# Turning normalized features through HBM instead of inside SBUF, and a bank-to-bank copy in the first gather, in a graph-attention kernel

## The chip, the core and the metric

The kernel runs on one core of one Trainium2 chip. The metric is the device time of one execution in microseconds. A core has five engines with instruction streams of their own: TensorE (PE) for matmuls, VectorE (DVE) and ScalarE (ACT) for element-wise work, GpSimd (POOL) and SyncE (SP). Here SP issues all plain DMAs and all DMA transpositions ("turns" below), and POOL issues the DMAs that add into their destination. All DMAs run on the same 16 DMA engines. SBUF is the on-chip memory, PSUM the matmul accumulators in 8 banks, HBM the memory outside.

## The reference

Inputs are x (32, 512, 512) and an adjacency (32, 512, 512) of integers: 32 samples of 512 nodes with 512 features. One pre-norm layer with two graph-attention (GAT) layers inside:

```python
def gat_layer(x, mask, W, a_src, a_dst, bias, concat):
    B, N, _ = x.shape
    H, F = a_src.shape
    xl = (x @ W).reshape(B, N, H, F)
    asrc = jnp.einsum('bnhf,hf->bnh', xl, a_src)
    adst = jnp.einsum('bnhf,hf->bnh', xl, a_dst)
    e = jax.nn.leaky_relu(asrc[:, :, None, :] + adst[:, None, :, :], NEG_SLOPE)
    e = jnp.where(mask[..., None], e, NEG_INF)
    attn = jax.nn.softmax(e, axis=1)
    out = jnp.einsum('bsdh,bshf->bdhf', attn, xl)
    out = out.reshape(B, N, H * F) if concat else out.mean(axis=2)
    return out + bias

h = jnp.maximum(_layernorm(x, axis=-1), 0.0)
mask = (adj > 0) | jnp.eye(N, dtype=bool)[None]
g = jax.nn.elu(gat_layer(h, mask, W1, att_src1, att_dst1, b1, concat=True))   # 4 heads of 256
x = x + gat_layer(g, mask, W2, att_src2, att_dst2, b2, concat=False)          # 1 head of 512
```

All data are float32.

## The kernel before

A sample goes through these stages: load of x, normalization and relu (`norm`, `norm_turn`), transposition of the normalized features into `ht` (features on partitions), projection with W1 (`project1`, into `xl`), scores and softmax of the four heads (`Soft.first`, `Soft.second`, weights in `p`), the weighted sums over neighbours (`gather1`, into `h1`, then `elu`), projection with W2 (`project2`), second softmax, second gather (`gather2`) and the store. All products of matrices are split into two-by-two blocks and done with seven block products in place of eight; the extra sums of blocks are made on DVE (`sums`, `sums1`, `sums2`, `low_sums`), and the seven products are added up partly inside a PSUM bank and partly by DVE.

The order of instructions is not the order of the code. Every function adds jobs (engine, cost in us, keys read, keys written) to a `Program`; PE's jobs keep the order of the code, and for the other engines the program searches an order with a model of costs, queues and DMA wires, then emits the instructions. SP's queue and POOL's queue are each one stream in that model. A job that turns by DMA has the size `prog.TURN` and is kept from overlapping with POOL's accumulating DMAs in the model (`crossed`). A key is the unit of dependence: a job waits for the last writer of what it reads, and for all readers of what it writes. Buffers come from small sets (`Slots`): four x tiles `xs`, two adjacency tiles `adjs`. `Banks` hands out the 8 PSUM banks; `take(width, kept)` with `kept` over 0 gives a free bank only if its last accumulation was at least that wide, so that a matmul may add to what another engine wrote there, and otherwise gives none.

The main loop (line 1698) runs over the samples, each iteration working on several: first gather of sample i+1 (heads 0 and 1), half of the projection of sample i+2, first gather (heads 2 and 3), the rest of the projection, second gather of sample i, load and norm of sample i+3, second projection of sample i+1, and `norm_turn` of sample i+3. So `ht` of a sample is needed when the next iteration's first half gather is over: `sums(ht_blocks())` and `low_sums()` on DVE read it, and `project1` on PE.

`norm_turn` (line 901) works on one block t of 128 nodes. ACT normalizes with relu in place (x tile `hn`). For samples 0 and 1, PE transposes. For all others the float32 words are split: ACT writes them as 16-bit halves, all low halves and then all high halves, into an adjacency tile (`words`, row adj<-x); SP issues a DMA transposition of 16-bit elements from there back into the x tile (`back`, row x<-adj); and ACT copies from `back` into `ht`, interleaving the halves again (row ht<-x). The same kind of DMA transposition turns the masks (row mt<-m, line 873), with `m` in SBUF as its source.

`gather1` (line 1437) takes two heads at a time in the order `PAIRS_OF`, and in the last iteration one by one in the order `SINGLY`. Product n of head h goes into the accumulator `ACC[n]`: 1, 6, 7 and 4 share bank "a", 5 and 3 bank "b", and 2 has a bank "g" of its own. After products 1, 4, 5, 6 ACT evicts the running sum into `h1` with the bias (row h<-mm,b_sb); after 2, 3, 7 DVE subtracts the bank from `h1` (row h<-h,mm). In `project1` a similar fork already stands: product 1 of the "low" block is copied by ACT into a second bank (row mm<-mm) if `Banks` has one wide enough. All instructions of a helper carry the helper's line: 646 for ACT, 649 for DVE, 652 for SP's plain DMAs, 657 for POOL's, 663 for matmuls.

Of the kernel before, what the change touches and what calls it, by code (L numbers as in the profile page):

```python
# [14 lines left out]
U16 = mybir.dt.uint16  # L15
AF = mybir.ActivationFunctionType
# [4 lines left out]
P = 128  # L21
# [491 lines left out]
def tile_gat(  # L513
# [37 lines left out]
    B, N, D = x.shape  # L551
# [15 lines left out]
    dram = ctx.enter_context(tc.tile_pool(name="dram", bufs=1, space=DRAM))  # L567

    def tiles(name, n, shape, dtype=F32, pool=sbuf):
        return [pool.tile(shape, dtype, name=f"{name}{i}") for i in range(n)]  # L570

    def slots(name, n, shape, dtype=F32, pool=sbuf):
        return Slots(name, tiles(name, n, shape, dtype, pool))
# [25 lines left out]
    ht = sbuf.tile([P, KT, N], F32, name="ht")  # L599
# [12 lines left out]
    ass = slots("as", 2, [P, 2, N])  # L612
    rrs = slots("rr", 2, [P, 2, N])
    das = slots("das", 2, [2 * NT, P], F32, dram)
    drs = slots("drr", 2, [2 * NT, P], F32, dram)
    mds = slots("dm", 3, [P, NT, N], BF16, dram)
    stats = slots("stats", 2, [P, NT, nc.vector.BN_STATS_DIM + nc.vector.BN_AGGR_DIM + 1])
# [2 lines left out]
    banks = Banks(tiles("mm", 8, [P, 512], F32, psum))  # L620
# [18 lines left out]
    def give_p(pk):  # L639
        if pk[0] == "p":  # L640
            ps_.give(pk)
# [3 lines left out]
    def act(cost, reads, writes, *a, **k):  # L645
        prog.add("ACT", cost, reads, writes, lambda: nc.scalar.activation(*a, **k))  # L646

    def dve(cost, reads, writes, f, *a, **k):
        prog.add("DVE", cost, reads, writes, lambda: f(*a, **k))  # L649

    def dma(size, reads, writes, to, at, cost=0.4):
        prog.add("SP", cost, reads, writes, lambda: nc.sync.dma_start(to, at), size)
# [7 lines left out]
    def pe(reads, writes, n, calls):  # L660
        def emit():
            for f, a, k in calls:
                f(*a, **k)  # L663

        prog.add("PE", n, reads, writes, emit)
# [235 lines left out]
    def norm_turn(b, t):  # L901

        (sk, st), (xk, hn) = ST[b], XT[b][t]
        S, A = nc.vector.BN_STATS_DIM, nc.vector.BN_AGGR_DIM
        act(
            0.71, [xk, sk + (t,)], [xk], hn, hn, AF.Relu,
            bias=st[:, t, S : S + 1], scale=st[:, t, S + A : S + A + 1],
        )
        if b < 2:
            pk, pt = banks.take()  # L910
            pe(
                [xk], [pk], 0.44,
                [(nc.tensor.transpose, (pt[:, k * P : (k + 1) * P], hn[:, k * P : (k + 1) * P], identf), {})
                 for k in range(KT)],
            )
            act(
                0.62, [pk], [("ht", t, 0), ("ht", t, 1)], ht[:, :, t * P : (t + 1) * P],
                pt.rearrange("p (k n) -> p k n", n=P), AF.Copy,
            )
            banks.give(pk)  # L920
        else:

            ak, a = adjs.take()
            words = a.bitcast(U16)
            act(
                0.96, [xk], [ak], words.rearrange("p (h f) -> p h f", h=2),
                hn.bitcast(U16).rearrange("p (f h) -> p h f", h=2), AF.Copy,
            )
            back = hn.bitcast(U16)
            prog.add(  # L930
                "SP", 1.3, [ak], [xk],
                lambda: nc.sync.dma_start_transpose(
                    back.rearrange("p (g n) -> p g n", n=P), words
                ),
                prog.TURN,
            )
            act(
                1.21, [xk], [("ht", t, 0), ("ht", t, 1)],
                ht[:, :, t * P : (t + 1) * P].bitcast(U16).rearrange("p k (n h) -> p h k n", h=2),
                back.rearrange("p (h k n) -> p h k n", h=2, n=P), AF.Copy,  # L940
            )
            adjs.give(ak)
        xs.give(xk)
        if t == NT - 1:
            stats.give(sk)
# [160 lines left out]
    M = N // 2  # L1106
# [273 lines left out]
    def sums1(h, pk, p, apart):  # L1380


        def a_block(i, j):
            return (
                xl[:, 2 * j : 2 * j + 2, h, 2 + i * P : 2 + (i + 1) * P],
                [("xl", 2 * j + k, h, i) for k in range(2)],
            )

        def b_block(r, c):
            return (  # L1390
                p[:, 2 * r : 2 * r + 2, c * M : (c + 1) * M], p_keys(pk, (2 * r, 2 * r + 1), (c,))
            )

        a11, a12, a21, a22 = (a_block(i, j) for i in range(2) for j in range(2))
        b11, b12, b21, b22 = (b_block(r, c) for r in range(2) for c in range(2))
        k = KQ + h % 2
        s1, s2 = (
            (hs[:, i, k, :].rearrange("p (k f) -> p k f", f=P), [("hs", i, k)]) for i in range(2)
        )
        s4 = s2  # L1400
        if apart:
            s4 = (hs4[:, h % 2, :].rearrange("p (k f) -> p k f", f=P), [("hs", 2, h % 2)])
        t1, t2 = (
            (t.rearrange("p (k f) -> p k f", f=M), [q]) for q, t in (ts_.take() for _ in range(2))
        )

        def op(cost, f, to, u, v):
            dve(cost, u[1] + v[1], to[1], f, to[0], u[0], v[0])

        add, sub = nc.vector.tensor_add, nc.vector.tensor_sub  # L1410
        op(0.34, add, s1, a21, a22)
        op(0.59, sub, t1, b12, b11)
        op(0.34, sub, s2, s1, a11)
        op(0.59, sub, t2, b22, t1)
        op(0.34, sub, a21, a11, a21)
        op(0.59, sub, b12, b22, b12)
        if apart:
            op(0.34, sub, s4, a12, s2)
        return (
            {1: a11, 2: a12, 3: s4, 4: a22, 5: s1, 6: s2, 7: a21},  # L1420
            {1: b11, 2: b21, 3: b22, 4: b21, 5: t1, 6: t2, 7: b12},
            lambda: op(0.59, sub, b21, b21, t2),
            (lambda: None) if apart else (lambda: op(0.34, sub, s4, a12, s2)),
        )
# [1 line left out]


    PAIRS_OF = tuple(
        tuple((h + i, n) for n in (1, 2, 6, 5, 7, 3, 4) for i in range(2)) for h in (0, 2)
    )  # L1430
    SINGLY = (
        (0, 1), (0, 5), (0, 2), (0, 6), (0, 3), (1, 1), (0, 7), (1, 5), (1, 2), (0, 4), (1, 6), (1, 3),
        (2, 1), (1, 7), (2, 5), (2, 2), (1, 4), (2, 6), (2, 3), (3, 1), (2, 7), (3, 5), (3, 2), (2, 4),
        (3, 6), (3, 3), (3, 7), (3, 4),
    )

    def gather1(soft, order):

        blocks, bank = {}, {}
        ahead = {h for h, n in order[:2]}  # L1440
        for h in sorted(ahead):
            blocks[h] = sums1(h, *soft.p[h], order is SINGLY)
        for h, n in order:
            if h not in blocks:
                blocks[h] = sums1(h, *soft.p[h], order is SINGLY)
            left, right, late, fourth = blocks[h]
            if n == 4:
                late()
            acc = ACC[n]
            first = n in (1, 2, 5)  # L1450
            if first:
                bank[h, acc] = banks.take(M)
            bk, bt = bank[h, acc]
            ps = bt[:, :M]
            (a, akeys), (w, wkeys) = left[n], right[n]
            pe(
                akeys + wkeys, [bk], KQ * M / 593,
                [
                    (mm, (ps, a[:, k, :], w[:, k, :]),
                     dict(start=(first and k == 0), stop=(k == KQ - 1), skip_group_check=True))  # L1460
                    for k in range(KQ)
                ],
            )
            if n == 6:
                fourth()
            r, c = BLOCK[n - 1]
            g = h * FPH + r
            to, key = h1[:, g, c * M : (c + 1) * M], ("h1", g, c)
            if n in (1, 4, 5, 6):
                act(  # L1470
                    COPY, [bk, "b1"], [key], to, ps, AF.Identity, bias=b1_sb[:, g : g + 1], scale=-1.0,
                )
            else:
                dve(ADD, [bk, key], [key], nc.vector.tensor_sub, to, to, ps)
            if n in (2, 3, 4):
                banks.give(bk)
            if n in (5, 6):
                ts_.give(right[n][1][0])

            if n in (3, 4):  # L1480
                elu(g)
            if n == 4:
                give_p(soft.p.pop(h)[0])
                yield h
# [160 lines left out]
    for t in range(NT):  # L1645
        norm_turn(0, t)
# [7 lines left out]
    for t in range(NT):  # L1654
        norm_turn(1, t)
# [37 lines left out]
    for t in range(NT):  # L1693
        norm_turn(2, t)
# [3 lines left out]
    for i in range(B - 1):  # L1698
# [17 lines left out]
        if front:  # L1716
# [6 lines left out]
            n = S1[i + 2] = Soft(i + 2, 1, scores_1)  # L1723
# [73 lines left out]
```

## Time and profile before

| what | us |
|---|---|
| median of 3 runs (lowest, highest) | 2760.99 (2758.34, 2761.75) |
| profiled execution, its own time | 2761.27 |
| its span, first to last instruction | 2759.5 |

The profiled execution is 0.28 us above the median of the runs. The granted TensorE clock was 0.999 over the span.

DMA moved 502.10 MB in 375,862 packets. Queue 1 (SP's) was on the wires for 43.7% of what 16 DMA engines could do in the span, queue 0 (POOL's) for 24.8%. The profile lists 120 DMA transpositions x<-adj and 64 mt<-m, 314 accumulating DMAs p<-dm that land 5.9 us after issue (median), 159 broadcasts rr<-drr and 159 small stores drr<-rr.

How the views are read: a row of the groups gives the line of the code, engine, operation, output<-input by name, shapes and the count; after the bar the busy time of the group in us and the mean duration of one in ns; after the second bar the engine's idle time before these instructions and what ended most of it. A row of the stages gives start:end and length in us, then busy time and number of instructions for PE, PE's weight loads, DVE, ACT and POOL, the granted clock, the DMA engines' busy share and GB/s. A float32 matmul is executed as two passes, so that the counts of PE are twice those in the code. A row of the timeline gives start and duration in us. SPq is SP's queue of DMA issues.

### The profile page before, as it was taken

How to read it: one execution, taken by the hardware profiler on the slowest of the kernel's cores; microseconds unless marked ns; L12 is line 12 of the kernel's file. 1: busy time of each engine (PE TensorE's matmuls, PEld its weight loads, DVE VectorE, ACT ScalarE, POOL GpSimd, SP SyncE). 2: the span in 40 equal slices, each digit the busy share in tenths (PEclk: the TensorE clock that was granted, in tenths of full speed). 3: DMA queues.
4: the chain of work that ended last, by engine and by line, in shares of the span. 5: the costliest groups of instructions: out<-in, count | busy, mean ns of one | idle time of the engine just before them, and what ended most of it. 6: DMA issues, size and time to landing. Idle time of an engine off the chain costs nothing.

```text
span 2759.5 us, 41946 instructions
## 1 busy us (share of the span) xinstructions
PE 2735.3 (99%) x12490; PEld 2365.6 (86%) x12490; DVE 2627.4 (95%) x6864; ACT 2244.0 (81%) x4751; POOL 323.8 (12%) x356
## 2 busy tenths in 40 slices
PE   7999999999999999999999999999999999999999
PEld 6688888888888888888888888888888888888887
DVE  8999999999999999999999999999999999999996
ACT  5978788888888788887889888888888898888883
POOL 0110111101111011101011110111111110101110
PEclk9999999999999999999999999999999999999999
DMA  8657766667666676776786667767667776668663
GB/s 233 176 153 181 206 178 172 182 179 202 180 184 178 177 184 188 187 183 169 187 204 184 172 178 191 190 184 188 171 180 181 200 189 165 181 183 210 165 172 107
DMA packets 375862, 502.10 MB, mean 182 GB/s; under 512 B 222804, under 2 KB 227668, under 8 KB 375636
## 3 DMA queue, kind: packets, MB, share of 16 engines
q1 hardware_dynamic: 329844, 332.68, 43.7%
q0 software_dynamic: 45792, 166.74, 24.8%
q8 instruction: 101, 1.65, 0.2%
q14 instruction: 125, 1.02, 0.1%
HBM read 316.41 MB, written 51.31 MB: 133 GB/s over the span
## 4 chain that ended last, share of the span: by engine, by line
PE 92%; DVE 3%; DMA 2%; ACT 2%; issue 1%; SPq 0%; DVEq 0%; ACTq 0%
PE mm L663 92%; ACT l L646 1%; DVE p L649 1%; DMA as<-das 0%; DMA adj<-in_adj_dram 0%; DVE h L649 0%; DMA rr<-drr 0%; DVE hs L649 0%; DMA p<-dm 0%; DVE w_sb L649 0%; ACT p L646 0%; DVE l L649 0%; DVE xr L649 0%; DVE t L649 0%; ACT xl L646 0%
## 5 line engine op out<-in xcount | busy, mean ns | idle before, releaser
L663 PE MATMUL mm<-w_sb,hs 128*128 128x257 f32 (+2 forms) x3032 | 697.5, 381 | 5.1 <-DVE hs L649 4.5
L663 PEld LDWEIGHTS mm<-w_sb,hs 128*128 128x128 f32 x3032 | 575.5, 190 | 91.4 <-DVE hs L649 6.1
L657 POOL DMA_DIRECT2D p<-dm x314 | 275.6, 887 | 2261.3 <-DVE p L649 1081.8
L646 ACT ACTIVATE l<-l,low 128x512 f32<-128x512 f32 x640 | 457.4, 717 | 16.0 <-DVE low L649 14.7
L663 PE MATMUL mm<-w_sb,h 128*128 128x257 f32 x2056 | 468.1, 379 | 0.7 <-ACT xl L646 0.7
L663 PE MATMUL mm<-p,xl 128*128 128x256 f32 (+1 forms) x1984 | 465.7, 382 | 0.0
L649 DVE SCALAR_TENSOR_TENSOR p<-rr,z 128x512 f32<-128x512 f32 (+1 forms) x636 | 454.7, 745 | 0.6 <-DMA rr<-drr 0.5
L646 ACT ACTIVATE l<-as,z 128x512 f32<-128x512 f32 x640 | 438.4, 714 | 17.2 <-DMA as<-das 16.6
L663 PEld LDWEIGHTS mm<-w_sb,h 128*128 128x128 f32 x2056 | 389.2, 189 | 59.1 <-ACT xl L646 1.1
L649 DVE CUSTOM_DVE_ANT_1 l<-l,mt 128x512 f32<-128x512 f32 x640 | 427.0, 686 | 7.3 <-ACT l L646 6.4
L663 PEld LDWEIGHTS mm<-p,xl 128*128 128x128 f32 x1984 | 376.8, 190 | 58.6 <-issue 6.9
L646 ACT ACTIVATE p<-p,z 128x512 f32<-128x512 f32 (+1 forms) x636 | 419.0, 716 | 9.6 <-DVE p L649 8.4
L663 PE MATMUL mm<-w_sb,ht 128*128 128x258 f32 x1802 | 421.3, 382 | 3.0 <-DVE xl L649 2.3
L646 ACT ACTIVATE h<-mm,b_sb 128x256 f32<-128x256 f32 (+1 forms) x504 | 232.3, 474 | 204.1 <-PE mm L663 201.8
L663 PEld LDWEIGHTS mm<-w_sb,ht 128*128 128x128 f32 x1802 | 340.1, 190 | 58.6 <-DVE xl L649 7.8
L646 ACT ACTIVATE xl<-mm 128x258 f32<-128x258 f32 (+2 forms) x686 | 253.4, 379 | 96.5 <-PE mm L663 93.3
L649 DVE TENSOR_TENSOR xl<-xl,mm 128x258 f32<-128x258 f32 (+1 forms) x526 | 215.4, 421 | 34.0 <-PE mm L663 29.0
L663 PE MATMUL mm<-t,hs 128*128 128x256 f32 x992 | 225.2, 379 | 0.0
L663 PEld LDWEIGHTS mm<-t,hs 128*128 128x128 f32 x992 | 188.5, 190 | 25.6
L646 ACT ACTIVATE xr<-h 128x512 f32<-128x512 f32 x256 | 158.4, 627 | 53.6 <-DVE h L649 52.6
L649 DVE TENSOR_TENSOR t<-mm,t 128x256 f32<-128x256 f32 (+1 forms) x424 | 172.3, 420 | 13.3 <-PE mm L663 11.9
L663 PE MATMUL mm<-xl,p 128*128 128x256 f32 (+1 forms) x752 | 179.4, 387 | 0.0
(132 smaller groups left out, 3475.1 us busy)
## 6 DMA issues: line engine op xcount, KB each, us to landing
p<-dm POOLq DMA_DIRECT2D x314, 512.0 KB, 5.9
rr<-drr SPq DMA_DIRECT2D x159, 512.0 KB
x<-in_x_dram SPq DMA_DIRECT2D x129, 256.0 KB
adj<-in_adj_dram SPq DMA_DIRECT2D x128, 256.0 KB
as<-das SPq DMA_DIRECT2D x64, 512.0 KB
t<-in_x_dram SPq DMA_DIRECT2D x124, 256.0 KB
out_dram<-t SPq DMA_DIRECT2D x124, 256.0 KB
dm<-m SPq DMA_DIRECT2D x64, 256.0 KB
```

The source lines that it names most:

```text
L646: prog.add("ACT", cost, reads, writes, lambda: nc.scalar.activation(*a, **k))
L649: prog.add("DVE", cost, reads, writes, lambda: f(*a, **k))
L657: lambda: nc.gpsimd.dma_start(to, at, accum_op=OP.add), size,
L663: f(*a, **k)
```

## The change

In `norm_turn`, for samples from 2 on, the halves in `words` are written by a plain DMA to a new HBM buffer `wd` (three of them, `dws`) of 256 rows by 512: row 2n is the low halves of node n, row 2n+1 the high halves. The DMA transposition then reads `wd` and writes `ht` directly: with nodes and halves together as rows, a low and a high half come to stand side by side, which is a float32 word. ACT's copy into `ht` is gone. The transposition waits for the write to HBM; the adjacency tile is read by the write instead of by the transposition.

In `gather1` with `PAIRS_OF`, ACT copies product 1 from its bank into a second bank in place of evicting it into `h1`, and product 2 accumulates on that copy; ACT then evicts the sum of 1 and 2 with the bias, in place of DVE's subtraction of 2 from `h1`. The order of the products goes from 1, 2, 6, 5, 7, 3, 4 to 1, 5, 6, 2, 7, 3, 4. If no bank fits, product 2 is handled as before. `SINGLY` stays as it was.

```diff
     das = slots("das", 2, [2 * NT, P], F32, dram)
+    dws = slots("dw", 3, [2 * P, D], U16, dram)
     drs = slots("drr", 2, [2 * NT, P], F32, dram)
...
                 hn.bitcast(U16).rearrange("p (f h) -> p h f", h=2), AF.Copy,
             )
-            back = hn.bitcast(U16)
+            wk, wd = dws.take()
+            dma(0.5, [ak], [wk], wd.rearrange("(n h) f -> n (h f)", h=2), words)
             prog.add(
-                "SP", 1.3, [ak], [xk],
+                "SP", 1.3, [wk], [("ht", t, 0), ("ht", t, 1)],
                 lambda: nc.sync.dma_start_transpose(
-                    back.rearrange("p (g n) -> p g n", n=P), words
+                    ht[:, :, t * P : (t + 1) * P].bitcast(U16), wd
                 ),
                 prog.TURN,
             )
-            act(
-                1.21, [xk], [("ht", t, 0), ("ht", t, 1)],
-                ht[:, :, t * P : (t + 1) * P].bitcast(U16).rearrange("p k (n h) -> p h k n", h=2),
-                back.rearrange("p (h k n) -> p h k n", h=2, n=P), AF.Copy,
-            )
+            dws.give(wk)
             adjs.give(ak)
...
-        tuple((h + i, n) for n in (1, 2, 6, 5, 7, 3, 4) for i in range(2)) for h in (0, 2)
+        tuple((h + i, n) for n in (1, 5, 6, 2, 7, 3, 4) for i in range(2)) for h in (0, 2)
...
-            first = n in (1, 2, 5)
+            first = n in (1, 5) or n == 2 and (h, "g") not in bank
             if first:
                 bank[h, acc] = banks.take(M)
...
-            if n in (1, 4, 5, 6):
+            fork = banks.take(M, M) if n == 1 and order is not SINGLY else None
+            if fork:
+                bank[h, "g"] = fork
+                act(0.29, [bk], [fork[0]], fork[1][:, :M], ps, AF.Copy)
+            elif n in (1, 4, 5, 6) or n == 2 and not first:
                 act(
                     COPY, [bk, "b1"], [key], to, ps, AF.Identity, bias=b1_sb[:, g : g + 1], scale=-1.0,
                 )
```

## The prediction

> **What bounds the kernel now.** I read the page's engine line first, then busy time by stage, then PE's waits, then the timeline around one turn.
>
> ```profile
> span 2759.5 us, 41946 instructions
> PE 2735.3 (99%) x12490; PEld 2365.6 (86%) x12490; DVE 2627.4 (95%) x6864; ACT 2244.0 (81%) x4751; POOL 323.8 (12%) x356
> ```
>
> A busy PE can hide waits, so the stages matter more (columns: stage, length, busy time with counts for each engine, granted clock, DMA share, GB/s):
>
> ```profile
> 0.00:86.00 86.00, 70.43 (x308) 58.77 (x309) 74.48 (x291) 54.00 (x114) 9.74 (x15) 0.98 0.82 233
> 86.00:2580.00 2494.00, 2491.19 (x11421) 2163.06 (x11420) 2400.60 (x6195) 2070.21 (x4381) 298.08 (x323) 1.00 0.69 182
> 2580.00:2759.50 179.50, 173.70 (x764) 143.76 (x762) 152.33 (x380) 119.76 (x258) 15.95 (x19) 1.00 0.55 152
> ```
>
> Between 86 and 2580 us PE is idle for 2494.0 - 2491.2 = 2.8 us in all, at a granted clock of 1.00. The other idle time is 15.6 us in the first 86 and 5.8 in the last 179.5. The timeline shows 16 passes of a 128x256 product in 3.45 us (1322.74 to 1326.19), 0.216 us each; full stages of 86 us hold 398 or 399 passes, and the sum of what the others lack is about 35 passes, 7.5 us with the 2.8 included. So the steady part can give back some 7 us and no more, and the change takes no matmul away. DVE, 96% busy there, is the next engine; ACT is at 83%, DMA at 0.69. What PE's matmuls wait for from 64 to 2580 us (total, times, longest):
>
> ```profile
> PE mm L663 <- ACT xl L646: 1.2, 2, 0.7
> PE mm L663 <- DVE xl L649: 1.0, 2, 0.6
> PE mm L663 <- DVE hs L649: 0.6, 2, 0.3
> ```
>
> **The change, part by part: the turn.** The rows that it touches:
>
> ```profile
> L646 ACT ACTIVATE ht<-x 128x1024 uint16<-128x1024 uint16 x120 | 161.3, 1362 | 2.9 <-DMA x<-adj 2.6
> L646 ACT ACTIVATE adj<-x 128x1024 uint16<-128x1024 uint16 x120 | 123.3, 1049 | 0.0
> L649 DVE TENSOR_TENSOR h<-h,mm 128x256 f32<-128x256 f32 x372 | 151.5, 419 | 1.8 <-PE mm L663 0.5
> L646 ACT ACTIVATE h<-mm,b_sb 128x256 f32<-128x256 f32 x496 | 227.0, 471 | 202.6 <-PE mm L663 200.3 <-DVE hs L649 0.8 <-DVE h L649 0.4
> ```
>
> *Removed:* the copy ht<-x, 120 times (30 samples by 4 blocks). Started back to back it holds ACT 1.21 us (1334.89 to 1336.10), so ACT loses 120 x 1.21 = 145 us. None of that is PE time.
>
> *Added:* 120 writes of 256 KB to HBM on SP's queue. The mask's write of the same size took SP 0.42 us to issue: 120 x 0.42 = 50 us for SP, which issues some 1,300 DMAs now and stands idle from 1301.8 to 1313.5 before sample 16's turn. On the wires, the packet records give 2 KB packets 102 ns on average; 128 of them over 16 engines are 0.81 us, so 120 writes are 98 us, 3.5% of the span.
>
> *Added wait:* the turn now waits on SP for its write to land. Behind it on SP stand the row and column broadcasts, the mask and x loads, the stores. The nearest rows are the small round trips through HBM: write issued at 1297.38, read back issued at 1301.44, 4.1 us; SP's longest wait for such a write is 3.8 us, for an adjacency load 6.3. I take 4.5 us from issue to landing (the small write's 4.1 plus half of the 0.81), with 3.5 and 6.8 as bounds.
>
> *Moved:* the turn reads HBM in place of SBUF; no row here does that. Its 1,024 packets of 256 B span 1.41 us (median of the 120 turns from SBUF; the mask's turns 1.6). Lower end 1.3, upper end twice the row, 2.8; I take 1.6, since the same bytes pass the same engines. The turn then lands in ht itself.
>
> The Trainium skill, DMA: Bandwidth & Descriptors, "Why small descriptors are slow (HBM only)", speaks against this: 256-byte pieces pay 3 cycles on 8 with HBM on one side, and copies inside SBUF are spared. An estimate from it is 1.41 x 11/8 = 1.94 us a turn; by it a sample's four turns cost the wires 2.1 us more, which adds nothing while the slack below lasts, and 30 x 0.5 = 16 us if the last turn always decides. No run so far shows which holds.
>
> *What this does to the deadline* shows at the last block of sample 16 (deinterleave on ACT, turn on SP, copy on ACT, first matmul on ht):
>
> ```profile
> 1327.32 1.04 ACT L646 ACTIVATE adj<-x 128x1024 uint16<-128x1024 uint16 x1
> 1328.38 1.24 SPq L932 DMA_TRANSPOSE x<-adj  x1
> 1334.89 1.34 ACT L646 ACTIVATE ht<-x 128x1024 uint16<-128x1024 uint16 x1
> 1334.82 2.34 PE L663 MATMUL mm<-w_sb,ht 128*128 128x258 f32 x10
> ```
>
> Old chain from 1328.4: 7.8 us to 1336.2, of which at least 3.66 (the shortest turn to copy of all 120) plus 1.36 are work, 5.0, and the rest is ACT's queue. New chain: write 4.5, turn 3.66 + 0.2, 8.4 us: 3.4 more work, 0.6 later than the 7.8 if nothing moves. But ACT has 4 x 1.21 = 4.8 us less to do in just this stretch, so the deinterleave can start up to 3.6 us earlier; and PE first reads ht a median 25 us after the sample's first normalization, of which the new chain with its two adjacency buffers (0.8 + 1.05 + 4.5 + 2 x 1.05 + 4.5 + 3.9 + the second turn's 1.3) needs 18. So I cost the turn at nothing on PE. If the cover goes, each microsecond late is a microsecond a sample, 30 in all: the first to wait are DVE's sums on ht, then project1's products.
>
> **First gather.** For 120 heads (30 samples by 4) ACT copies product 1 bank to bank in place of evicting it, product 2 accumulates on the copy, and one eviction of the sum takes the place of the subtraction h<-h,mm. So evictions stay 496, DVE loses 120 x 0.42 = 50 us, and ACT gains one copy a head. The only PSUM-to-PSUM copy in the trace took 0.364 us; ACT is held about 0.27 of such a length (a copy at 706.83, the next start at 707.09): 120 x 0.27 = +32 us, and ACT ends 145 - 32 = 113 us lighter. PE's instructions are the same. The waits: product 6 adds into product 1's bank, so ACT must have read it. Between the two stand three products, 3 x 0.86 = 2.6 us, before and after (1, 2, 6 against 1, 5, 6); ACT's work there falls from 2 x 0.36 to 2 x 0.27 us for a pair of heads. Product 2 now waits for the copy too, five products or 4.3 us after product 1. If ACT is held by two 0.7 us exponentials the copies still end after 1.9 us: nothing on PE. With four it is 0.7 us late, once a pair, 60 pairs, 42 us; but ACT idled 200 us before these evictions waiting for PE, so I take 0, with +2 as its part of the range. Banks: 6 of 8 held at most.
>
> **Sum.** Own time of the profiled execution 2761.3 (span 2759.5 and 1.8 around it), 0.3 over the runs' median. Gain: half of the 2.8 us of steady idle time, as DVE and ACT get lighter: -1.4. Turn 0, gather 0, start and end 0. 2759.9, on the median's footing **2759.6 us**.
>
> **Rivals.** *A, the DMA crowds and ht comes late: slower.* Its place is the stretch in which turn, mask loads and exponent masks meet:
>
> ```profile
> 1310.00:1320.00 10.00, 10.00 (x48) 8.71 (x47) 9.26 (x28) 10.00 (x21) 2.41 (x3) 1.00 0.93 228
> 1320.00:1330.00 10.00, 10.00 (x48) 8.78 (x47) 9.01 (x25) 8.92 (x15) 0.00 (x0) 1.00 0.66 157
> 1330.00:1340.00 10.00, 9.89 (x47) 8.34 (x46) 9.85 (x23) 8.90 (x18) 3.45 (x4) 1.00 1.09 259
> ```
>
> Mean DMA share 0.89: 3.2 us free of 30, while four writes bring 3.2 and slower HBM turns 0.8 to 5.6. It decides once the last turn lands over about 3 us later than in my chain; half a microsecond of PE per sample is 15 us, 2775, one is 2790. Against it: over a whole sample (86 us at 0.69) 26 us of wire are free, and stores and x loads can move. *B, the freed engines let a new order close the gaps: faster.* All 2.8 us go, and about 3 of the 4.3 us wait for hs at 52.7 us in the start, and 1 near the end: 2761.0 - 6.8 = 2754. Against it: the first 12 us of PE idle are the first load, and samples 0 and 1 are turned by PE, untouched. *C, the order computed for all instructions falls otherwise at start and end,* where PE idles 21.4 us: a few us either way, say +6, 2767. *D, the fork finds no bank* of the needed width and the old subtraction stays (project1's own fork shows as one copy in the whole trace): DVE stays at 95%, time 2761.
>
> **Numbers.** Forecast with D 0.53, A 0.20, B 0.19, C 0.08. I call 0.2%, 5.5 us, no change: below 2755.5 is faster, above 2766.5 slower. Forecast alone: 2756 to 2765. For 8 in 10 the range reaches into B and A: **2752 to 2779**. Faster 0.19, within 0.53, slower 0.28.
>
> **What would show it.** No ht<-x on ACT; ACT near 2130 us (120 copies of 0.364 for 120 of 1.362), DVE near 2577, h<-h,mm at 252, a new copy mm<-mm some 120 times, h<-mm,b_sb still 496; PE's busy time unchanged within 3 us and idle 86 to 2580 us under 5. Turn: write-to-turn waits on SP under 6.8 us and DMA share near 0.73. Wrong if PE's waits for DVE hs or hl, or for the turn's DMA, sum to more than 5 us (A), or if the first 86 us change by more than 3 (B, C).

## The result, and the profile after

The changed kernel takes 2823.02 us (median of 4 runs, 2817.51 to 2825.34), against 2761.09 before: 1.022 times as long, 95% interval 1.0208 to 1.0232. That is 62 us more, 2.1 us for each of the 30 samples that are turned by DMA. The forecast was 2759.6 us, no change.

The page's engine line of the changed kernel:

```profile
span 2821.5 us, 41988 instructions
PE 2755.9 (98%) x12490; PEld 2361.5 (84%) x12490; DVE 2594.4 (92%) x6744; ACT 2152.8 (76%) x4751; POOL 322.4 (11%) x356
```

Both engines that were to be relieved were: DVE is busy 33 us less and ACT 91 us less. PE has the same 12,490 passes to do. Yet the kernel is slower. Busy time by stage (the same columns as before: PE, weight loads, DVE, ACT, POOL, clock, DMA share, GB/s):

```profile
0.00:86.00 86.00, 70.51 (x314) 57.80 (x315) 73.97 (x291) 50.84 (x112) 8.20 (x14) 1.00 0.84 236
86.00:2580.00 2494.00, 2449.39 (x11131) 2106.46 (x11130) 2308.79 (x5926) 1939.98 (x4275) 290.32 (x315) 1.00 0.70 190
2580.00:2821.50 241.50, 236.03 (x1049) 197.22 (x1047) 211.68 (x529) 162.00 (x365) 23.89 (x27) 1.00 0.60 163
```

In the start and in the rest PE idles as long as before (15.5 and 5.5 us); the loss is in the steady part. In the same 2,494 us PE now idles 44.6 us (2.8 before) and makes 290 passes less, which at 0.216 us each is 62.6 us: the whole loss. The idle time shows 41.8 us of it; the rest is in PE's busy time over the span, which has grown by 20.6 us. The waits over the span (engine and line, what it waited for: total, times, longest):

```profile
DVE hl L650 <- DMA ht<-dw: 51.7, 23, 4.3
PE mm L664 <- DVE h L650: 17.7, 17, 1.9
PE mm L664 <- DVE hs L650: 12.2, 15, 2.0
```

The same three rows in the kernel before, where ACT's copy stands for the turn:

```profile
DVE hl L649 <- ACT ht L646: 1.5, 3, 0.6
PE mm L663 <- DVE h L649: 0.5, 1, 0.5
PE mm L663 <- DVE hs L649: 4.8, 3, 4.3
```

The long wait in the first row is new: 23 times DVE stands still for up to 4.3 us until a turn lands. DVE starts nothing else in that time (the timeline below shows one such stop of 2.93 us), so that what PE needs, the subtractions on h and the sums hs, stands behind. The groups that the change touches:

```profile
L647 ACT ACTIVATE mm<-mm 128x256 f32<-128x256 f32 x120 | 44.4, 372 | 16.0 <-PE mm L664 15.0 <-DVE p L650 0.5
L647 ACT ACTIVATE h<-mm,b_sb 128x256 f32<-128x256 f32 x496 | 231.1, 470 | 218.1 <-PE mm L664 216.2 <-DVE z L650 0.4 <-DVE t L650 0.4
L650 DVE TENSOR_TENSOR h<-h,mm 128x256 f32<-128x256 f32 x252 | 100.9, 412 | 2.4 <-PE mm L664 1.7
L650 DVE TENSOR_TENSOR hl<-ht 128x128 f32<-128x128 f32 x31 | 8.9, 287 | 35.0 <-DMA ht<-dw 28.7 <-DMA das<-as 5.7 <-issue 0.6
L650 DVE TENSOR_TENSOR hl<-hl,ht 128x128 f32<-128x128 f32 x31 | 8.8, 284 | 16.9 <-DMA ht<-dw 16.9
L650 DVE TENSOR_TENSOR hl<-ht,hl 128x128 f32<-128x128 f32 x31 | 8.8, 284 | 6.1 <-DMA ht<-dw 6.0
```

Every count is as the change says. The last three rows are the place: the three small sums on `ht` (`low_sums`, line 700). The first has 35 us of idle time ahead of 8.9 us of work, the other two 23 us together. In the kernel before, waits ahead of them came to 1.5 us in all.

**One sample in the timeline** (sample 21: third turn, DVE before and after its wait, fourth turn, the next stall of PE):

```profile
1795.09 1.25 SPq L934 DMA_TRANSPOSE ht<-dw  x1
...
1796.75 0.22 DVE L650 TENSOR_SCALAR z<-xl,c 128x4 f32<-128x4 f32 x1
1799.90 0.29 DVE L650 TENSOR_TENSOR hl<-ht 128x128 f32<-128x128 f32 x1 [2.93 <-DMA ht<-dw]
1800.77 0.28 DVE L650 TENSOR_TENSOR hl<-ht,hl 128x128 f32<-128x128 f32 x1
...
1801.47 1.25 SPq L934 DMA_TRANSPOSE ht<-dw  x1
...
1805.06 2.13 PE L664 MATMUL mm<-p,xl 128*128 128x256 f32 x8 [1.08 <-DVE h L650]
```

The small sums read blocks 0 and 1. By the DMA packet records those two turns had ended by 1792.9. The packets of the third turn, block 2, end at 1799.3, and only then, at 1799.9, DVE goes on. So DVE waits for a block that it does not read. And the fourth turn is issued right after the third small sum: over the 30 samples it follows the end of that sum by 0.0 to 0.7 us in 24. It waits for a sum that does not read its block either.

The list of waits in the built program says the same. For sample 16 (DMAHW n is the n-th of eight completion semaphores that SP's DMAs use in turn; rows of DVE and of SP):

```
3153 hl<-ht 128x128               [waits DMAHW4, DMAHW1, DMAHW0]
689  turn ht<-dw_119 (first)      completes on DMAHW0
690  turn ht<-dw_117 (second)     completes on DMAHW1
693  turn ht<-dw_118 (third)      completes on DMAHW4
700  turn ht<-dw_119 (fourth)     [waits DMAHW7, DMAHW3, DVE]
```

In one partition, `ht` holds for each of the four feature groups the 512 nodes in a row; a block of 128 nodes is thus four pieces with those of the other blocks between them. The waits are placed as if a turn wrote everything from its first piece to its last. That is inferred from which waits are there. Over the 30 samples one of the three small sums waits for the third or fourth turn in 28 (the first of them in 23), and the third or fourth turn waits for DVE in 29. ACT's copies, which wrote the same pieces in the kernel before, bring none of this: in the list of that kernel none of the 120 waits for DVE, and no small sum waits for a copy of block 2 or 3. The searched order knows only the keys ("ht", t, c), and by these there is nothing to wait for: the order was made for a program without these waits.

### The profile page after: what moved, and what is told of

The parts are those of the page before. It is cut to its first block, busy times and chain, and to the rows that moved or that the text cites. A ratio compares the mean times of both kernels' runs of the same rounds, so it can differ in the third digit from the quotient of the medians.

```text
span 2821.5 us, 41988 instructions
## 1 busy us (share of the span) xinstructions
PE 2755.9 (98%) x12490; PEld 2361.5 (84%) x12490; DVE 2594.4 (92%) x6744; ACT 2152.8 (76%) x4751; POOL 322.4 (11%) x356
## 5 line engine op out<-in xcount | busy, mean ns | idle before, releaser
L664 PE MATMUL mm<-p,xl 128*128 128x256 f32 (+1 forms) x1984 | 473.5, 387 | 17.1 <-DVE h L650 17.0
```

## The experiments

The runs below were taken together with new runs of the kernel before (medians 2762.85 us for the first four, 2763.38 us for the last four); each ratio is to those.

Theory W: these false waits are the loss. Rival S: the three HBM buffers, since the fourth write reuses the first one's and waits until the first turn has read it. Rival C: the DMA crowding of the prediction. Rival G: the gather's bank copy.

**The turn alone and the gather alone** (each part of the diff undone).

> The turn through HBM alone; the first gather as before. Theory W (false waits: DVE's first sum on ht waits for a third turn whose block it doesn't read, and the fourth turn waits for that sum): nearly the whole loss is here, 2810 to 2840 us, DVE hl waiting 40 us or more on DMA ht<-dw. Rival S (three HBM buffers: the fourth write waits for the first turn) and rival C (DMA crowding) say the same time. Rival G (the gather's bank copy delays PE): 2765 us or less.

Measured: 2864.42 us, ratio 1.0366 (1.0339 to 1.0393), more than both parts together and above the 2810 to 2840 us that W had said: the order is another one, and W missed the size. The wait that W names is there, and G has no part in this run. DVE's wait for the turns is longer than in the change:

```profile
DVE hl L650 <- DMA ht<-dw: 89.8, 31, 8.6
```

> The bank-to-bank copy and the new order of products alone; the turn as before. Theory W, S and C: no loss, 2750 to 2762 us, DVE near 2577 us, as a subtraction goes per head. Rival G: 2790 us or more, PE waiting for ACT's copies mm<-mm or for DVE h.

Measured: 2755.12 us, ratio 0.9969 (0.9958 to 0.9981): a gain, and G falls. In the steady part PE idles for nothing:

```profile
86.00:2580.00 2494.00, 2494.00 (x11454) 2170.72 (x11453) 2376.86 (x6103) 2119.83 (x4521) 300.06 (x325) 1.00 0.70 183
```

**Eight HBM buffers**, with `ht` as it was.

```diff
-    dws = slots("dw", 3, [2 * P, D], U16, dram)
+    dws = slots("dw", 8, [2 * P, D], U16, dram)
```

> The changed kernel with eight HBM buffers in place of three, so that no write waits for an earlier turn to have read its buffer; the searched order changes with it. Theory W: the false waits stay, 2790 to 2825 us, DVE hl still waiting 30 us or more on DMA ht<-dw. Rival S: nearly all comes back, 2765 us or less. Rival C: unchanged, 2815 to 2830.

Measured: 2886.43 us, ratio 1.0449 (1.0433 to 1.0465), outside what any theory had said. The order is another one, and in it DVE meets the false waits more often:

```profile
DVE hl L650 <- DMA ht<-dw: 127.5, 40, 7.4
```

A real wait is gone, and the ratio is 0.023 higher, which speaks against S; but the order has changed with it, so this run alone does not decide. It fits W, since the search places turns and sums by its keys alone and cannot see which places bring a false wait.

**`ht` in halves of nodes**, three buffers as in the change.

```diff
-    ht = sbuf.tile([P, KT, N], F32, name="ht")
+    ht = sbuf.tile([P, 2, KT, N // 2], F32, name="ht")
...
-                    ht[:, :, t * P : (t + 1) * P].bitcast(U16), wd
+                    ht[:, t // 2, :, t % 2 * P : (t % 2 + 1) * P].bitcast(U16), wd
```

> The changed kernel with ht laid out as two halves of nodes, each contiguous in a partition (blocks 0 and 1, then 2 and 3), in place of blocks interleaved by feature group: same jobs, same searched order, same DMAs; only waits between blocks of different halves fall away. Theory W: most of the 62 us comes back, 2762 to 2785 us, DVE hl waiting under 15 us on DMA ht<-dw. Rivals S and C: 2810 us or more. Rival G: 2810 us or more.

Measured: 2769.21 us, ratio 1.002 (1.001 to 1.0029) where the change had 1.022. The sequences of instructions on all five engines are the same as in the changed kernel. In the list of waits, row 3153 has lost DMAHW4 and row 700 has lost DVE. The same place in sample 21:

```profile
1751.19 1.25 SPq L934 DMA_TRANSPOSE ht<-dw  x1
...
1752.98 0.28 DVE L650 TENSOR_TENSOR hl<-ht 128x128 f32<-128x128 f32 x1
1753.84 0.29 DVE L650 TENSOR_TENSOR hl<-ht,hl 128x128 f32<-128x128 f32 x1
...
1754.53 2.07 SPq L934 DMA_TRANSPOSE ht<-dw  x1
```

The small sum starts 1.8 us after the third turn is issued, long before it can have landed (its last packet is at 1756.1), and the idle time ahead of it is gone; no row of the waits names hl and the turn any more:

```profile
L650 DVE TENSOR_TENSOR hl<-ht 128x128 f32<-128x128 f32 x31 | 8.6, 278 | 0.0
```

S and C fall as the main cause: buffers, transfers and order are those of the change, and the kernel is within 0.2% of the one before. W is shown.

**Halves and eight buffers.**

> ht in halves and eight HBM buffers together. Theory W with S as its remainder (the fourth write waits for the first turn, which reads the buffer it reuses): 2745 to 2760 us, PE idle under 3 us between 86 and 2580 us. If only W is true: 2762 to 2772 us, as with three buffers. Rival C (DMA crowding as remainder): 2765 to 2775 us.

Measured: 2756.98 us, ratio 0.9975 (0.9965 to 0.9984). With the eight-buffer order (the same sequences of instructions on all engines), the layout alone takes the ratio from 1.0449 to 0.9975. Steady part, first with three buffers, then with eight:

```profile
86.00:2580.00 2494.00, 2485.79 (x11393) 2156.72 (x11392) 2363.99 (x6071) 1983.97 (x4372) 297.25 (x322) 1.00 0.74 194
```

```profile
86.00:2580.00 2494.00, 2491.77 (x11439) 2167.50 (x11438) 2374.05 (x6094) 1993.08 (x4399) 301.87 (x325) 1.00 0.74 195
```

PE's idle time goes from 8.2 to 2.2 us, and SP's waits for the write to land from 37.8 to 6.3 us. Since the order changes with the buffers, S's share of the last 12 us is likely but not separated.

**The turn alone, with halves.**

> The turn through HBM with ht in halves, the first gather as before. Theory W: far below the turn alone with interleaved blocks (1.037 times before): 2765 to 2790 us, DVE hl waiting under 10 us on DMA ht<-dw. If the false waits were not the cause of that loss: 2840 us or more.

Measured: 2783.89 us, ratio 1.0077 (1.006 to 1.0095), against 1.0366 with blocks interleaved, and no wait of DVE hl on a turn is left. It is the third pair with one order and two layouts, and the third in which the layout takes the loss away, here most of it. In none of the three kernels in halves does a small sum wait for the third or fourth turn, or a turn for DVE, in the list of waits. The 0.8% that is left here is not explained. Its steady part shows PE idle for 17.8 us:

```profile
86.00:2580.00 2494.00, 2476.24 (x11320) 2146.13 (x11319) 2386.90 (x6145) 1930.58 (x4234) 294.77 (x321) 1.00 0.73 193
PE mm L664 <- DVE hs L650: 14.9, 7, 8.4
```

About half of it is the one wait of 8.4 us.

**The order of products alone, and the layout alone.**

> Only the order of products in the first gather (1, 5, 6, 2, 7, 3, 4), without the bank copy. If the gather's gain comes from DVE's 120 fewer subtractions: 2759 to 2766 us, no gain. If the order alone gives it: 2752 to 2757 us.

Measured: 2764.16 us, ratio 1.0002 (0.9993 to 1.0011): nothing. So the gather's 0.3% comes with the bank copy, which takes 120 subtractions from DVE.

> The gather's part alone with ht in halves, ACT's copy into ht as before: a control for the layout. Theory W: as the gather's part alone, 0.997 times before, 2750 to 2759 us, as ACT's copies brought no waits between blocks. If the layout itself saves time: 2745 us or less.

Measured: 2755.93 us, ratio 0.9972 (0.9963 to 0.9981), as the gather alone with `ht` as it was. So the layout is worth nothing where ACT writes `ht`; what it repairs are waits that only the turn brought.

Fastest are the gather's part alone (0.9969) and both parts with halves and eight buffers (0.9975); their intervals overlap. So even mended, the turn through HBM brings no time: ACT is 130 us less busy (2282.5 against 2152.7), and ACT was not what PE waited for (1.2 us from 64 to 2580 us in the kernel before).

## Why the prediction was wrong

**The step that failed** is "So I cost the turn at nothing on PE", with its slack of 25 us against 18 as cover. The durations in the chain were about right; the dependences were not. The prediction took them from the keys in the code, where small sums on blocks 0 and 1 need two turns and the fourth turn needs only its write. The program that runs has two more: a small sum waits for the third turn, and the fourth turn waits for a small sum. With the turn at nothing the change lost 62 us, and the turn alone, in its own order, 102 us. The third turn's landing stalls DVE, which is 92% busy, and the fourth cannot start until DVE has passed.

**Rival A had the size but not the mechanism.** "One is 2790" per microsecond a sample gives 2823 for the 2.1 us found. But the DMA engines were not crowded: with the same transfers the loss is gone in halves. Its sign did come: it named waits of PE for DVE hs or hl, or for the turn's DMA, above 5 us in sum, and they are 12.2 and 0.7 us. But PE's larger wait is for the subtractions on h (17.7 us), and the wait behind both, DVE's own on hl with 51.7 us, it did not name.

**The price of the turn was right.** From HBM its packets span 1.50 us from first to last in the median, against 1.6 taken and 1.43 from SBUF; from issue to last packet it is 3.2 us against 3.0. (The prediction's 1.41 and 1.6 for the turns from SBUF are no spans but the packets' time shared out over 16 engines; the spans are 1.43 and 1.9.) In the engines' time a turn is 1.31 us in the median and 1.63 in the mean, against 1.41 and 1.61 from SBUF, and the median packet of 256 B takes 18 ns in both, so there is no penalty for small pieces from HBM here. The estimate of 1.94 us from the Trainium skill, DMA: Bandwidth & Descriptors, "Why small descriptors are slow (HBM only)", is not borne out here. In the 13 turns where the trace shows a wait for the turn's own write, the write landed 4.6 us after its issue in the median (2.5 to 6.3), where 4.5 was taken; SP's longest wait for a write was 4.7 us, under the 6.8 that was named.

**The gather was right in its counts, and taken at nothing it was under-sized.** 120 copies at 0.372 us, 496 evictions, 252 subtractions, and in the gather alone no wait of PE for a copy. Alone it gives 0.3%, about 8 us: the 2.8 us of steady idle time and some 5 us that the profile counted as busy (PE 2730.4 us against 2735.3), where half of 2.8 was taken. The stage count of some 7 us to be had was the better bound.

**Engine times.** DVE fell by 33 us, not 50, ACT by 91, not 113: the sums were 17 and 22 us too large, and neither term entered the forecast time. The runs of one part show where: the turn alone takes 132 us from ACT, not 145, and the gather alone adds 38 us, not 32; for DVE the sum took the full 0.42 us of a subtraction, and the gather alone frees 33 us for 120 of them, 0.28 each.

**Rivals B, C and D:** the freed engines did close the gaps, but only in the gather's part alone, where PE idles for nothing in the steady part. In the change the idle time in the first 86 us went from 15.6 to 15.5 us, so nothing moved there. The fork found its bank all 120 times.

## What to carry to other kernels

When a transfer takes over a write from an engine, read in the built program which waits stand on its destination: here blocks strided through a tile waited for, and held up, neighbours that they did not touch. Lay blocks that are written and read at different times contiguously. A scheduler that plans with finer dependences than the build enforces can plan into such waits, and here DVE, over 90% busy, passed them on to PE. And taking 130 us of work from ACT, which PE did not wait for, paid nothing.

## What was not expected of the hardware

A 16-bit turn with HBM as its source cost the DMA engines no more than one inside SBUF (for 256 KB 1.31 us against 1.41 in the median, 1.63 against 1.61 in the mean).

The granted TensorE clock over the span was lower where PE stalled more often: 0.999 before, 0.997 for the change, 0.991 for the turn alone, 0.988 with eight buffers and `ht` interleaved (PE idle for 2.8, 44.6, 68.0 and 78.2 us in the steady part), and 1.000 for the gather alone and for both parts with halves and eight buffers (0 and 2.2 us). In the change the clock record shows four stretches of 3.41 us at half clock between 1008 and 1726 us, each within 1.3 us after an idle gap of PE of 1.9 to 2.2 us. For the change the 0.002 are at most 0.002 x 2,821 = 6 of its 62 us.
